# A three-layer graph network on one core: 20 instead of 18 node blocks of layer 1 by count matrices

## The chip, the cores and the metric

The kernel runs on one core of a Trainium2 chip. The metric is the time of one execution on the device, in microseconds (us). A core has five engines with one instruction queue each: PE multiplies matrices, DVE and ACT work on rows of elements, POOL here issues the indirect transfers (gathers), SP and ACT issue the plain ones. An engine carries out its instructions in the order in which they were written and waits for others by semaphores.

## What is computed

Three graph convolutions on 6250 nodes with 256 features and 100,000 edges, sorted by destination, then a residual and a layer norm. With a self loop at each node, `deg` counts the edges that end in a node:

```python
dinv = jnp.where(deg > 0, jax.lax.rsqrt(deg), 0.0)
norm_edge = dinv[src] * dinv[dst]
h = x
for W, b in ((W1, b1), (W2, b2), (W3, b3)):
    # _gcn_layer
    h = h @ W
    msg = h[src] * norm_edge[:, None]
    agg = jax.ops.segment_sum(msg, dst, num_segments=n_nodes)
    h = jax.nn.relu(agg + b)
return _layernorm(x + h)
```

The widths are 256 -> 512 -> 512 -> 256. The kernel sums over the edges first and multiplies by the weights after that, where this is narrower.

## The kernel before, in words

**Blocks and chunks.** The nodes are cut into 50 blocks of `Q` = 125. The edges that end in a block (some 2000) are `KF` = 16 chunks of 128 edges; what goes beyond is gathered once per ten blocks. The sum of a block's incoming rows is made in one of two ways.

*Gathered.* For each chunk, POOL gathers 128 rows of the layer's table from DRAM into a row buffer (L853). PE multiplies them with a 0/1 matrix `shot` of 128 edges by 125 nodes (L879), which DVE makes by comparison, four chunks at a time (L822). For a part of the chunks the row is split into a rounded half (ACT, L894) and the rest (DVE, L897), so that one faster matmul does the work; in layer 1 that is every second chunk. L866 starts a block: it adds the block's own rows (the self loop).

*Dense.* A block's incoming edges are counted in a matrix of 125 destinations by 6250 sources, held as bytes. ACT (in layer 3 at times DVE) converts five 125x125 pieces at a time (L830), and PE multiplies all 50 pieces with the nodes' features, which stay on chip as `parts`, 512 wide (L922). L913 starts such a block.

**Layers.** `layer(i, ...)` writes out one layer, step by step; a step is one chunk of the gathered blocks. Layer 1 (i = 0) gathers blocks `FEW` to 49 and has the first `FEW` = 18 dense. Layer 2 (i = 1) gathers all 50. Layer 3 gathers 22 and has `MANY` = 28 dense. With the gathers per ten blocks, these are 516, 805 and some 354 steps. Each step writes out, in this order: the gather of a chunk, the split of the chunk before it and of one further back, the product of the chunk `lag` = 4 steps back, whatever finishing steps of blocks (`after1` to `after3`) have come due, then the extras (below), then as many dense matmuls as the step's share. In layer 1 the dense share is spread evenly by `spacing` from step 28 to 12 steps before the end: 1.89 matmuls a step.

**Making count matrices.** `counts` makes the matrices from the edges in groups of five destination nodes, 25 groups (`GB`) to a block. For a group, PE multiplies two 0/1 matrices (L727) and ACT copies the product, 125x250, out of PSUM into the byte matrix (L732). The 0/1 matrices come from three comparisons on DVE for five groups together (L705). After the 25th group the matrix is stored to DRAM in `kept` (SP). `fetching_few` fetches it back when two earlier ones are used up, and marks it usable ten steps later. Layer 1 makes the matrices that it uses itself; the other ten (18 to 27) are made in layer 2, a new one every 74 steps. `counts` is a generator; every `yield` ends its share of a step. The argument `rush` is `GB` in layer 1 and 0 in layer 2: in layer 1 the first 25 groups go two to a step, all others, and all in layer 2, one to a step.

**PSUM.** The product of a group goes to one of three places in turn, `mat_places`: two halves of the bank `mat_ps`, and the upper half of the bank `near`. The lower half of that bank is `near_cols`, a table of numbers that DVE reads in all comparisons (L705 and L822).

**Edge windows.** While layer 1 begins, `windows` fetches the edges for the groups, 125 groups at a time, with small operations on DVE, PE, ACT and POOL.

**Row buffers.** In layer 1 there are 25 for the chunks, so POOL can issue that far ahead of their use.

Layer 2 gathers from the table that the finished blocks of layer 1 write, so its first gather waits for the last of them.

Of the kernel before, what the change touches and what calls it, by code (L numbers as in the profile page):

```python
# [37 lines left out]
SPLIT = ((1, 2, 4), (1, 2, 4), (3, 4, 6))  # L38


FEW = 18
MANY = 28
G = 5
GB = Q // G
# [6 lines left out]
def by_rows(queue, tile_rows, dram_rows, store=False):  # L51

    for s in (slice(0, EVEN), slice(EVEN, Q)):
        if store:
            queue.dma_start(out=dram_rows[s], in_=tile_rows[s])
        else:
            queue.dma_start(out=tile_rows[s], in_=dram_rows[s])
# [320 lines left out]
def sorted_path(ctx: ExitStack, tc: tile.TileContext, x, edges, starts, found, wts, biases, room, late, out):  # L378
# [318 lines left out]
    def counts(blocks, places, rush=0):  # L697

        def compared(out, numbers):
            shape = list(out.shape)
            nc.vector.tensor_tensor(out, near_cols[:, :shape[2]].unsqueeze(1).to_broadcast(shape),  # L705
                                    numbers.unsqueeze(2).to_broadcast(shape), op=ALU.is_equal)

        hot = {}
        total = len(blocks) * GB
        for s in range(total + 5):  # L710
            if s < total and s % GB == 0:
                while (blocks[s // GB] + 1) * GB > seen * Q:
                    yield 1
            if s < total and s % WIDE == 0:
                t, w = divmod(blocks[s // GB] * GB + s % GB, Q)
                hot_lo = pairs.tile([P, WIDE, Q], BF16, name="hot_lo")
                hot_key = pairs.tile([P, WIDE, G * NB], BF16, name="hot_key")
                hot[s // WIDE] = hot_lo, hot_key
                compared(hot_lo, slots[:, t, 0, w:w + WIDE])
                compared(hot_key[:, :3], slots[:, t, 1, w:w + 3])  # L720
            if s < total and s % WIDE == 2:
                t, w = divmod(blocks[s // GB] * GB + s % GB + 1, Q)
                compared(hot[s // WIDE][1][:, 3:], slots[:, t, 1, w:w + WIDE - 3])
            m = s - 4
            if 0 <= m < total:
                hot_lo, hot_key = [h[:, m % WIDE] for h in hot[m // WIDE]]
                nc.tensor.matmul(mat_places[m % 3], lhsT=hot_lo, rhs=hot_key, start=True, stop=True)  # L727
            m = s - 5
            if 0 <= m:
                n, u = divmod(m, GB)  # L730
                place = places[n % len(places)]
                nc.scalar.copy(place[:, :, u * G:(u + 1) * G], mat_places[m % 3].rearrange("p (k r) -> p k r", r=G))  # L732
                if u == GB - 1:
                    by_rows(nc.sync, place.rearrange("p k v -> p (k v)"), kept[blocks[n]], store=True)
                    stored.append(blocks[n])
            if s >= rush or s % 2:
                yield 1


# [328 lines left out]
    now = 0  # L1068
    few, many, every = list(range(FEW)), list(range(MANY)), list(range(NB))

    seen = 2

    def steps(b):

        return (NB - b) * KF + NG - b // GRP

    def all_windows():
        nonlocal seen
        for t in range(seen, NW):
            yield from windows(t)  # L1080
            seen += 1

    def fetching_few():

        for m, b in enumerate(few):
            while b not in stored or finished < m - 1:
                yield 1
            fetch(b, now + 10)

    first = 28  # L1090
    spacing = (steps(FEW) - first - 12) / FEW
    layer(0, C, every[FEW:], few, after1, first_rows, first, spacing, [(0, all_windows()), (1, counts(few, (made, also_made), GB)), (1, fetching_few())])

    def last_weights():
        load_w2()
        load_w3()
        yield 1
# [3 lines left out]
    split = two.enter_context(tc.tile_pool(name="swide_split", bufs=4))  # L1101
    gap = (steps(0) - 60) // (MANY - FEW)
    layer(1, HID, every, [], after2, wide_rows,
          extras=[(5, last_weights())] + [(10 + gap * n, counts([b], (made,))) for n, b in enumerate(many[FEW:])])
    there.clear()
    fetch(many[0], 6)
# [189 lines left out]
```

## Time and profile before

| | |
|---|---|
| median of 3 runs | 2350.66 us (2350.42 to 2360.2) |
| the profiled execution | 2345.07 us, span 2343.4 us |
| PE busy (matmul) | 1995.7 us, 85% of the span |
| POOL busy | 1668.6 us, 71% |
| DVE busy | 1540.3 us, 66% |
| ACT busy | 1253.3 us, 53% |
| first gather of layers 1, 2, 3 | 97.58, 796.62, 1873.57 us |
| last gather of layer 1 | 776.13 us |

By stage, busy time of each engine inside a stretch well within layers 1, 2 and 3, from the view of windows:

| stretch, us | PE | DVE | ACT | POOL | DMA share |
|---|---|---|---|---|---|
| 150 to 700 | 484.28 | 378.39 | 347.79 | 402.75 | 0.58 |
| 850 to 1800 | 821.28 | 626.03 | 489.93 | 727.89 | 0.78 |
| 1900 to 2300 | 393.87 | 292.94 | 231.97 | 305.64 | 0.69 |

A line of a group reads: source line, engine, operation, output<-inputs, shape, count, then busy time and mean duration of one in ns, then the engine's idle time ahead of it and what ended that. A line of a timeline reads: start, duration, engine, line, operation, output<-inputs, shape, count, and in brackets the idle time before it and its releaser. A matmul's duration includes its way through the array, so matmuls that follow each other overlap, and the duration of one is more than its price in a row of many. Lines that begin with a time, a duration and an engine with a tile but no operation are from the chain of waits: there the duration is the time that passed on the chain.

### The profile page before, as it was taken

The numbers are of one execution on the slowest core, as the hardware profiler recorded it, in microseconds if no ns is written. First come the engines' busy times: TensorE is split into PE (matmuls) and PEld (weight loads), VectorE is DVE, ScalarE is ACT, GpSimd is POOL, SyncE is SP. The second block draws the span as 40 slices with busy tenths as digits, with TensorE's granted clock in tenths as the row PEclk, the third lists the DMA queues.
The fourth block names the chain that finished last, engine by engine and source line by source line (L and its number), as shares of the span: only waits on it lengthen the run. The fifth ranks groups of instructions, "written<-read, shape, count | busy, mean of one in ns | idle before, by whom it ended". The sixth has DMA issues, their size and how long they took to land.

```text
span 2343.4 us, 29386 instructions
## 1 busy us (share of the span) xinstructions
PE 1995.7 (85%) x7965; PEld 1377.6 (59%) x7965; DVE 1540.3 (66%) x2923; ACT 1253.3 (53%) x2777; POOL 1668.6 (71%) x1716
## 2 busy tenths in 40 slices
PE   3378889889889778988879888898889889999997
PEld 2256656566657335555546555555555667777785
DVE  5677766667664466676666766767665357777776
ACT  1456566666665355555555555545554355555664
POOL 2277677777767577777777777777777377777776
PEclk9989999999999889999999999998999989999998
DMA  8355565566555577777777877777777556676664
GB/s 182 109 152 147 163 192 161 170 181 175 149 165 152 148 228 224 228 235 221 235 226 226 236 221 237 220 228 237 217 232 222 150 154 171 185 184 183 180 181 131
DMA packets 178080, 447.61 MB, mean 191 GB/s; under 512 B 43347, under 2 KB 75429, under 8 KB 177904
## 3 DMA queue, kind: packets, MB, share of 16 engines
q0 software_dynamic: 107456, 326.24, 49.0%
q1 hardware_dynamic: 55328, 107.63, 15.8%
q10 hardware_dynamic: 15120, 11.77, 2.0%
q8 instruction: 64, 1.05, 0.2%
q14 instruction: 112, 0.92, 0.1%
HBM read 391.61 MB, written 53.88 MB: 190 GB/s over the span
## 4 chain that ended last, share of the span: by engine, by line
PE 41%; DMA 25%; DVE 13%; issue 8%; ACT 6%; POOL 4%; ACTq 0%; POOLq 0%; DVEq 0%; SPq 0%
DMA room<-tab,ssrc 16%; PE sacc L879 13%; PE sacc L922 10%; DMA spare<-tab,ssrc 8%; PE smm L969 3%; DVE hot_key L705 3%; DVE halves L897 3%; PE mat_ps L922 3%; PE win_ps L922 3%; ACT halves L894 3%; POOL room L853 3%; PE win_ps L1009 3%; DVE shot L822 2%; PE smm L1026 2%; DVE hot_lo L705 1%
## 5 line engine op out<-in xcount | busy, mean ns | idle before, releaser
L853 POOL DMA_INDIRECT room<-tab,ssrc x1032 | 1016.5, 985 | 317.3 <-issue 138.9
L879 PE MATMUL sacc<-halves,shot 128*125 128x512 f32 x1808 | 734.8, 462 | 82.5 <-DVE halves L897 50.3
L853 POOL DMA_INDIRECT spare<-tab,ssrc x632 | 617.8, 978 | 198.8 <-issue 87.1
L897 DVE TENSOR_TENSOR halves<-room,halves 128x512 fp32r<-128x512 f32 (+1 forms) x746 | 417.4, 565 | 379.9 <-ACT halves L894 368.2
L894 ACT CAST halves<-room 128x512 fp32r<-128x512 f32 (+1 forms) x746 | 381.5, 518 | 341.5 <-DMA room<-tab,ssrc 229.2
L879 PEld LDWEIGHTS sacc<-halves,shot 128*125 128x125 f32 x1808 | 331.5, 192 | 328.1 <-DVE halves L897 110.3
L922 PE MATMUL sacc<-parts,piece 125*125 125x512 f32 x1400 | 476.3, 431 | 10.1 <-ACT piece L830 10.1
L897 DVE TENSOR_TENSOR halves<-spare,halves 128x256 fp32r<-128x256 f32 (+1 forms) x462 | 248.4, 544 | 213.0 <-ACT halves L894 204.6
L879 PE MATMUL sacc<-room,shot 128*125 128x512 f32 (+1 forms) x780 | 332.3, 509 | 11.8 <-DMA room<-tab,ssrc 11.7
L822 DVE TENSOR_TENSOR shot<-near_cols,sdlo 128x500 fp32r<-128x500 f32 x443 | 297.6, 672 | 45.7 <-ACT room L732 23.4
L894 ACT CAST halves<-spare 128x256 fp32r<-128x256 f32 (+1 forms) x462 | 229.2, 503 | 180.5 <-DMA spare<-tab,ssrc 131.2
L922 PEld LDWEIGHTS sacc<-parts,piece 125*125 125x125 f32 x1400 | 236.2, 190 | 92.8 <-issue 30.6
L830 ACT CAST piece<-room 125x625 fp32r<-125x625 uint8 x376 | 268.1, 714 | 41.4 <-DVE piece L830 10.3
L732 ACT CAST room<-mat_ps 125x250 uint8<-125x250 f32 x470 | 197.6, 438 | 167.4 <-PE mat_ps L727 165.7
L705 DVE TENSOR_TENSOR hot_key<-near_cols,slots 128x750 bf16<-128x750 f32 (+1 forms) x280 | 224.2, 801 | 14.7 <-ACT room L732 8.5
L1009 PE MATMUL win_ps<-room,w_sb 128*128 128x250 f32 x800 | 212.2, 390 | 1.6 <-ACT room L1017 0.9
L727 PEld LDWEIGHTS <-hot_lo 128*125 128x125 bf16 x700 | 98.9, 142 | 172.8 <-DVE hot_key L705 102.8
L1009 PEld LDWEIGHTS win_ps<-room,w_sb 128*128 128x128 f32 x800 | 160.4, 201 | 49.6 <-issue 23.7
L732 ACT CAST room<-near_cols 125x250 uint8<-125x250 f32 x230 | 100.7, 438 | 146.3 <-DVE hot_key L705 86.5
L879 PEld LDWEIGHTS sacc<-room,shot 128*125 128x125 f32 x780 | 144.4, 195 | 46.8 <-DMA room<-tab,ssrc 14.1
L727 PE MATMUL near_cols<-hot_key,hot_lo 128*125 128x250 bf16 x230 | 67.8, 295 | 115.0 <-DVE hot_key L705 87.7
L727 PE MATMUL mat_ps<-hot_key,hot_lo 128*125 128x250 bf16 x470 | 131.0, 281 | 11.5 <-ACT room L732 11.3
(181 smaller groups left out, 1985.7 us busy)
## 6 DMA issues: line engine op xcount, KB each, us to landing
room<-kept SPq DMA_DIRECT2D x46, 683.6 KB
kept<-room SPq DMA_DIRECT2D x28, 683.6 KB
tab<-st SPq DMA_DIRECT2D x75, 224.0 KB
room<-tab,ssrc POOLq DMA_INDIRECT x1032
spare<-tab,ssrc POOLq DMA_INDIRECT x632
spare<-tab SPq DMA_DIRECT2D x43, 224.0 KB
out<-st ACTq DMA_DIRECT2D x50, 112.0 KB
room<-in_x ACTq DMA_DIRECT2D x4, 1120.0 KB
```

The costliest lines, as they stand in the source:

```text
L705: nc.vector.tensor_tensor(out, near_cols[:, :shape[2]].unsqueeze(1).to_broadcast(shape), numbers.unsqueeze(2).to_broadcast(shape), op=ALU. ...
L727: nc.tensor.matmul(mat_places[m % 3], lhsT=hot_lo, rhs=hot_key, start=True, stop=True)
L732: nc.scalar.copy(place[:, :, u * G:(u + 1) * G], mat_places[m % 3].rearrange("p (k r) -> p k r", r=G))
L822: nc.vector.tensor_tensor(hot[:, :n], near_cols[:, :Q].unsqueeze(1).to_broadcast([P, n, Q]), dlo.rearrange("p b j -> p (b j)")[:, at:at + ...
L830: convert(piece, used[m % 2][:, c * PIECE:(c + 1) * PIECE, :])
L853: nc.gpsimd.indirect_dma_start(out=row, out_offset=None, in_=tables[i], in_offset=bass.IndirectOffsetOnAxis(ap=at, axis=0))
L879: nc.tensor.matmul(acc[:Q, :size], lhsT=hot, rhs=row[:, c0:c0 + size], start=(i == 1 and k == c0 == 0), stop=(k == KF and c0 + size == row ...
L894: nc.scalar.copy(halves[:, :width], landed[chunk - hi_lag])
L897: nc.vector.tensor_sub(halves[:, width:], landed.pop(chunk - lo_lag), halves[:, :width].bitcast(F32))
L922: nc.tensor.matmul(acc_d[:Q], lhsT=got[done // PIECE][:, k % PIECE, :], rhs=parts[:, k], start=False, stop=(k == NB - 1))
L969: nc.tensor.matmul(y_ps, lhsT=zt[:, k, :], rhs=w1_sb[:, k, :], start=(k == 0), stop=(k == KC - 1))
L1009: nc.tensor.matmul(h_ps[:, f, :], lhsT=w2_sb[:, k, (f2 + f) * P:(f2 + f + 1) * P], rhs=zt2[:, k, :], start=(k == 0), stop=(k == KH - 1))
```

## The change

Two blocks of layer 1 move from the gathered to the dense way (`FEW`), and with them the making of their two count matrices moves from layer 2 to layer 1. In layer 1, from the 26th group on, a step carries a second group whenever the group's number is a multiple of eight, so that eight groups go in seven steps. Layer 1 has 483 steps and 20 dense blocks, 2.26 dense matmuls a step; layer 2 makes eight matrices, one every 93 steps. Layer 3 is as before.

```diff
-FEW = 18
+FEW = 20
 MANY = 28
...
     def counts(blocks, places, rush=0):
...
                 if u == GB - 1:
                     by_rows(nc.sync, place.rearrange("p k v -> p (k v)"), kept[blocks[n]], store=True)
                     stored.append(blocks[n])
-            if s >= rush or s % 2:
+            if s % 2 if s < rush else s % 8 or not rush:
                 yield 1
```

The places where `FEW` counts, unchanged:

```python
first = 28
spacing = (steps(FEW) - first - 12) / FEW
layer(0, C, every[FEW:], few, after1, first_rows, first, spacing, [(0, all_windows()), (1, counts(few, (made, also_made), GB)), (1, fetching_few())])
...
gap = (steps(0) - 60) // (MANY - FEW)
layer(1, HID, every, [], after2, wide_rows,
      extras=[(5, last_weights())] + [(10 + gap * n, counts([b], (made,))) for n, b in enumerate(many[FEW:])])
```

## The prediction

> **What bounds the kernel now.** I read the chain and the groups of the page first, and they name the gathers: POOL's indirect DMAs are the costliest group, and gathered rows head the chain of waits. So I took the time per stage, in the timeline of POOL.
>
> ```profile
> L853 POOL DMA_INDIRECT room<-tab,ssrc x1032 | 1016.5, 985 | 317.3 <-issue 138.9
> ...
> 415.43 0.95 POOL L853 DMA_INDIRECT room<-tab,ssrc  x1 [0.30 <-PE mat_ps L727]
> 416.68 0.94 POOL L853 DMA_INDIRECT room<-tab,ssrc  x1 [0.30 <-DVE hot_key L705]
> ...
> 641.70 0.94 POOL L853 DMA_INDIRECT room<-tab,ssrc  x1 [1.48 <-PE mat_ps L727]
> ```
>
> A gather is issued every 1.25 us and each carries 0.30 us of fixed gap, whatever releaser is named. In layers 2 and 3 no gather waits longer than that 0.31 us (the first ones apart), so POOL sets their pace. In layer 1 some do wait, for PE, between 618 and 710 us. POOL runs up to 25 row buffers ahead there; a wait means that the buffers are used up and PE is the slower one. PE's own pace is read from its timeline at L866, the first matmul of each gathered block:
>
> ```profile
> 134.54 0.77 PE L866 MATMUL sacc<-parts,ident_r 125*125 125x512 f32 x1
> 157.67 0.40 PE L866 MATMUL sacc<-parts,ident_r 125*125 125x512 f32 x1
> ...
> 706.52 0.39 PE L866 MATMUL sacc<-parts,ident_r 125*125 125x512 f32 x1
> 723.22 0.39 PE L866 MATMUL sacc<-parts,ident_r 125*125 125x512 f32 x1
> ...
> 774.64 0.40 PE L866 MATMUL sacc<-parts,ident_r 125*125 125x512 f32 x1
> ```
>
> The first and the third line are 26 blocks apart: 572.0 / 26 = 22.0 us a block, while POOL needs 16.1 x 1.25 = 20.1 us. From 706.52 to 774.64 it is 4 blocks in 68.1, 17.0 us each. What ends at 708 us is the making of count matrices (L727's last matmul there). So while counts are made, the layer goes at PE's pace, and the counts cost 5.0 us per block of 16.1 groups: 0.31 us a group. Bare, a count matmul takes 0.11 to 0.24 us on PE (chain of waits, 178.60 and 179.83 us). The rest is waiting, and the groups by form from 150 to 700 us say where:
>
> ```profile
> L727 PE MATMUL mat_ps<-hot_key,hot_lo 128*125 128x250 bf16 x270 | 73.5, 272 | 1.7 <-ACT room L732 1.5
> L727 PE MATMUL near_cols<-hot_key,hot_lo 128*125 128x250 bf16 x135 | 38.9, 288 | 41.2 <-DVE hot_key L705 35.6 <-DVE shot L822 4.0 <-ACT room L732 0.8
> ```
>
> Two of the three places of a count product lie in mat_ps and wait for nothing; the third shares a bank with near_cols, which DVE reads in every comparison, and there PE loses 41.2 of the roughly 66 us that it idles in these 550. That bank ties PE, DVE and ACT together once every three groups.
>
> The Trainium skill says of this (PSUM — Partial Sum Buffer, "PSUM bank collisions raise a hardware error") that the scheduler adds a dependency between any two instructions on different engines that touch one bank and quadrant, reads against reads too, even at different columns. The trace agrees as far as it goes, with 41.2 us of waiting at that place against 1.7 at the two others. By that rule the wait belongs to the group, not to the block, and the sum is the first of the two below (+27); without it the second (+18) would be as good.
>
> **The change, part by part.** Times are of the profiled execution (span 2343.4, 2345.07 us in all), which is 5.6 us under the median of the runs shown, 2350.66.
>
> *Removed from layer 1:* two gathered blocks, 33 gathers (483 steps instead of 516). At POOL's 1.25 that is 41 us of issuing, but POOL is not the bound while counts are made, so what counts is PE's share. *Added:* 2 dense blocks of 50 matmuls, 50 count groups, one group more per seven steps. In the order of the built program a gathered block then carries 18.4 count groups and 36.2 dense matmuls instead of 16.1 and 30.4, and the counts end 25.6 blocks after the block that starts at 134.54, with 2.4 left, instead of 26 and 4.
>
> Prices on PE, from the chain where nothing holds it:
>
> ```profile
> 180.31 1.72 PE smm L969 x4
> 182.03 0.23 PE sacc L913
> 182.26 0.24 PE sacc L922
> ```
>
> A dense matmul 0.235, times 5.8 = 1.36 us a block. Its bounds are 0 (it fills a wait) and the 0.44 of its mean duration in this stage; I take the bare one, since PE issues it back to back. The finishing of dense blocks: 0.72 instead of 0.61 per gathered block, each 4 x 0.43 + 2 x 0.19 + 0.23 = 2.3 us, so +0.25. A count group 0.31, with 0.11 (bare) below and 0.84 above (before any dense block runs, the block from 109.29 to 134.54 takes 25.2 us for 30 groups, two per step; there DVE is the limit). I take 0.31, as the rows of this very stage give it.
>
> A block with counts after: 17.0 + 1.36 + 0.25 + 18.4 x 0.31 = 24.3 us; without: 18.6. From 134.54 to the start of the last block: 25.6 x 24.3 + 2.4 x 18.6 = 667 us, against 640 now: +27. The 22 us from there to the first gather of layer 2 (774.64 to 796.62) stay. If the waits stay as they are per block and only the bare 0.11 to 0.24 of each further group is added, a block takes 22.0 + 1.61 + 2.3 x 0.15 = 23.96 and it is +18. I take the middle, **+22 us**.
>
> *Moved out of layer 2:* 50 groups, some 7 us of count matmuls on PE and 50 casts on ACT. Costed at nothing, since gathers pace that layer; in the windows the first and the third stretch have 20 count matmuls each, the others none:
>
> ```profile
> 1005.00:1035.00 30.00, 22.99 (x24) 0.94 0.73 207
> 1050.00:1080.00 30.00, 22.70 (x25) 0.94 0.78 234
> 1105.00:1135.00 30.00, 23.28 (x23) 1.00 0.75 217
> 1150.00:1180.00 30.00, 22.99 (x24) 0.94 0.78 229
> ```
>
> POOL issues 24, 25, 23 and 24 gathers in 30 us (columns: busy, count, PE clock, DMA share, GB/s). Were the difference of one gather real, 10 stretches of some 35 us would hide about 14 us, and two fewer are worth 3. The spread also comes from where the window cuts; I keep 0 to -3.
>
> *Queues:* SP gets two stores and two fetches of matrices more in layer 1 and two stores fewer in layer 2, 0.75 us of issuing each. Behind them in order stand the stores of finished rows, which layer 2 alone reads. What can hurt is lateness: a matrix must be stored, fetched and landed before ACT converts its first piece, and ACT, then PE, would stand still for it. Now this slack grows from 10 steps for the first matrix to over 30; after, it stays at 10 to 17 (a matrix is made in 21.9 steps and used in 22.15). In the timeline of SP a store at 164.99 is followed by its fetch at 169.43, and the first piece is converted at 177.87: at most 13 us, under 10 steps x 1.4. Cover is thin, price 0; a fetch that is held up behind other stores (306.99 to 315.68) would miss by about 4 us, and some eight matrices have no more slack: up to +30.
>
> Layer 3 and the start are not touched. Sum: 2345 + 22 = 2367 on the profiled execution, 2373 on the median; I write 2371.
>
> **The rivals.**
> 1. *Gathers pace layer 1 after all* (or a block with counts still takes 22.0 us): 33 x 1.25 = 41 us less, or 25.6 x 22.0 + 2.4 x 17.0 = 604 instead of 640, 36 less: about 2311. It decides once a block with counts takes less than 20.1 us on PE. For it: the page's chain and POOL's group. Against: PE lags POOL by all buffers from 618 us on, and blocks take 17.0 us as soon as counts stop.
> 2. *The added work fills PE's waits.* PE idles 66 of 550 us, 2.6 us a block; if the added 2.0 us go half into it, a block takes 23.0 and the sum is 25.6 x 23.0 + 2.4 x 18.6 = 633, 7 less: about 2341. For it: DVE is late at the shared bank, and gets more time per step. Against: DVE also gets 14% more comparisons per step, and work per three groups hardly changes on any engine (three groups then span 2.62 steps instead of 3).
> 3. *The doubled step hurts*, or the fetches come late: in every eighth group two products follow each other with only one cast between them, two of the three places being one bank. At 0.84 us for such a group instead of 0.31, 60 of them add 32 us: 2403. For it: the block at 109.29. Against: there DVE also makes windows.
> 4. *No change of the work*: excluded, the built program has 33 gathers fewer, 500 count matmuls in layer 1 and 200 in layer 2.
>
> **How the numbers follow.** Forecast 0.59, rival 1 0.13, rival 2 0.17, rival 3 0.11. A change under 0.5% (12 us) is not told from none here: within that lie rival 2 and a little of the forecast's lower edge, 0.19; faster is rival 1 and a rest, 0.14; slower 0.67. The range holds the forecast with both prices of a group, rival 2 with a larger share filled (another 5 us), and rival 3: 2338 to 2402. Rival 1 is left out. The likeliest alone: 2360 to 2388.
>
> **What would show it.** L866 in PE's timeline about 24 us apart until some 750 us and 18 to 19 after; the first gather of layer 2 near 818 instead of 796.62; waits of POOL for PE from early in layer 1, near 60 us in all (33 x 1.25 + 22); idle time of near_cols L727 up by a tenth. Layers 2 and 3 as long as now: 1076.9 us from first gather to first gather, and 469.8 from 1873.57 to the end. Wrong if blocks stay at 22 us (rival 1), if near_cols idles less while blocks take 23 (rival 2), if waits appear on mat_ps or before L830 (rival 3), or if layer 2 changes its length by more than 5 us.

## The result and the profile after

The changed kernel takes 2373.19 us (median of 8 runs, 2363.61 to 2381.18) against 2353.41 us of the kernel before (8 runs beside it, 2350.42 to 2360.2): a ratio of 1.0082 with a 95% interval of 1.0059 to 1.0105, or +19.8 us. The profiled execution took 2374.55 us. The page of the kernel after gives its span and the busy time, share and instructions of each engine:

```profile
span 2372.9 us, 29390 instructions
PE 2018.6 (85%) x8013; PEld 1384.6 (58%) x8013; DVE 1532.3 (65%) x2899; ACT 1262.1 (53%) x2781; POOL 1645.3 (69%) x1683
```

PE's share is 85%, as before, so this part of the page tells nothing. The stages do. From the timeline of POOL in the kernel after, the first gather that waited for PE, the last gather of layer 1, and the first of layers 2 and 3:

```profile
416.80 1.00 POOL L853 DMA_INDIRECT room<-tab,ssrc  x1 [1.14 <-PE mat_ps L727]
...
789.77 1.11 POOL L853 DMA_INDIRECT room<-tab,ssrc  x1 [0.31 <-issue]
818.63 0.95 POOL L853 DMA_INDIRECT room<-tab,rest  x1 [27.75 <-issue]
...
1899.33 0.95 POOL L853 DMA_INDIRECT room<-tab,rest  x1 [30.55 <-DMA tab<-st]
```

With the first gather of all at 97.40, the stages of the two profiled executions are:

| us | before | after | difference |
|---|---|---|---|
| first gather of layer 1 to that of layer 2 | 699.0 | 721.2 | +22.2 |
| layer 2 to layer 3 | 1076.9 | 1080.7 | +3.8 |
| layer 3 to the end | 469.8 | 473.5 | +3.7 |

The change does nothing in layer 3, so I take the 3.7 us there for what such a stage varies by from one execution to the next, and layer 2's 3.8 can't be told from it. The spans of these two executions differ by 29.5 us and the medians by 19.8, so I take layer 1's 22.2 as known to some 4 us, not to tenths. The loss is in layer 1. PE's timeline at L866, the first matmul of each gathered block, after:

```profile
134.94 0.48 PE L866 MATMUL sacc<-parts,ident_r 125*125 125x512 f32 x1
...
739.74 0.40 PE L866 MATMUL sacc<-parts,ident_r 125*125 125x512 f32 x1
758.19 0.40 PE L866 MATMUL sacc<-parts,ident_r 125*125 125x512 f32 x1
776.41 0.40 PE L866 MATMUL sacc<-parts,ident_r 125*125 125x512 f32 x1
796.94 0.39 PE L866 MATMUL sacc<-parts,ident_r 125*125 125x512 f32 x1
```

The first two lines are 25 blocks apart: 604.8 / 25 = 24.19 us a block with counts, where it was 22.0. The three blocks behind take 18.45, 18.2 and 20.5 us, 19.1 on average, where it was 17.0.

POOL's side of the same layer is a ledger, from the start times of its gathers: their number less one times the median distance, the waiting beyond that, and the time from the last gather to the first of layer 2.

| us | issuing | waiting | last gather to layer 2 | sum |
|---|---|---|---|---|
| before | 515 x 1.251 = 644.3 | 34.3 | 20.5 | 699.0 |
| after | 482 x 1.254 = 604.4 | 87.9 | 28.9 | 721.2 |

Two blocks less to gather took 40 us of issuing away; 54 us of waiting came in, and 8 at the end. The waits view of POOL from 100 to 800 us names for whom it waited, after (total, times, longest in us; 0.3 of each is the fixed gap of a gather):

```profile
POOL w_sb L464 <- DVE w_sb L461: 22.5, 4, 10.2
POOL spare L853 <- PE sacc L879: 16.5, 19, 2.5
...
POOL room L853 <- PE sacc L879: 15.1, 18, 2.5
POOL room L853 <- PE mat_ps L727: 12.7, 15, 2.7
POOL spare L853 <- PE near_cols L727: 11.7, 13, 2.1
```

All lines of this view that name PE sum to 87.1 us over 119 waits; without the gap, 51 us. In the kernel before it is 49.1 over 131, so 10 us. The row buffers are used up from 417 us on instead of 618: PE lags from there. The first line is a wait of the edge windows' fetches, which stand in POOL's queue between the gathers; it was 11.7 us.

### The profile page after: what moved, and what is told of

Read it like the earlier page. It is cut to its first block, busy times and chain, and to the rows that moved or that the text cites. A ratio compares the mean times of both kernels' runs of the same rounds, so it can differ in the third digit from the quotient of the medians.

```text
span 2372.9 us, 29390 instructions
## 1 busy us (share of the span) xinstructions
PE 2018.6 (85%) x8013; PEld 1384.6 (58%) x8013; DVE 1532.3 (65%) x2899; ACT 1262.1 (53%) x2781; POOL 1645.3 (69%) x1683
## 4 chain that ended last, share of the span: by engine, by line
DMA 26%; PE 25%; DVE 7%; issue 6%; ACT 5%; POOL 3%; ACTq 0%; SPq 0%; POOLq 0%; DVEq 0%
DMA room<-tab,ssrc 17%; PE sacc L879 8%; DMA spare<-tab,ssrc 8%; PE sacc L922 5%; PE mat_ps L922 3%; ACT halves L894 3%; DVE halves L897 3%; PE win_ps L922 2%; PE win_ps L1009 2%; POOL room L853 2%; PE smm L1026 1%; DVE shot L822 1%; DVE hot_key L705 1%; PE smm L969 1%; POOL spare L853 1%
## 5 line engine op out<-in xcount | busy, mean ns | idle before, releaser
L853 POOL DMA_INDIRECT room<-tab,ssrc x1016 | 1008.8, 993 | 336.4 <-issue 142.1
L853 POOL DMA_INDIRECT spare<-tab,ssrc x616 | 603.0, 979 | 213.2 <-issue 76.8
L897 DVE TENSOR_TENSOR halves<-room,halves 128x512 fp32r<-128x512 f32 (+1 forms) x790 | 449.5, 574 | 389.1 <-ACT halves L894 383.2
L894 ACT CAST halves<-room 128x512 fp32r<-128x512 f32 (+1 forms) x790 | 410.3, 526 | 413.3 <-DMA room<-tab,ssrc 288.0
L897 DVE TENSOR_TENSOR halves<-spare,halves 128x256 fp32r<-128x256 f32 (+1 forms) x402 | 208.6, 524 | 224.7 <-ACT halves L894 213.0
L822 DVE TENSOR_TENSOR shot<-near_cols,sdlo 128x500 fp32r<-128x500 f32 (+1 forms) x435 | 291.6, 670 | 41.6 <-ACT room L732 26.4
L922 PEld LDWEIGHTS sacc<-parts,piece 125*125 125x125 f32 x1500 | 252.4, 190 | 98.0 <-issue 36.2
L830 ACT CAST piece<-room 125x625 fp32r<-125x625 uint8 x396 | 282.1, 714 | 40.7 <-DVE halves L897 9.4
L879 PE MATMUL sacc<-room,shot 128*125 128x256 f32 (+1 forms) x656 | 269.7, 494 | 11.1 <-DMA room<-tab,ssrc 11.1
L894 ACT CAST halves<-spare 128x256 fp32r<-128x256 f32 (+1 forms) x402 | 193.0, 488 | 141.2 <-DMA spare<-tab,ssrc 99.3
L705 DVE TENSOR_TENSOR hot_key<-near_cols,slots 128x750 bf16<-128x750 f32 (+1 forms) x280 | 224.1, 801 | 20.9 <-ACT room L732 13.0
L727 PEld LDWEIGHTS <-hot_lo 128*125 128x125 bf16 x700 | 96.7, 140 | 157.9 <-DVE hot_key L705 91.2
L879 PE MATMUL sacc<-spare,shot 128*125 128x256 f32 (+1 forms) x428 | 180.9, 505 | 2.5 <-DMA spare<-tab,ssrc 2.4
L727 PE MATMUL near_cols<-hot_key,hot_lo 128*125 128x250 bf16 x230 | 67.2, 292 | 101.2 <-DVE hot_key L705 75.6
L879 PEld LDWEIGHTS sacc<-room,shot 128*125 128x125 f32 x656 | 122.0, 195 | 39.7 <-DMA room<-tab,ssrc 12.0
```

Source lines behind the costliest of these rows:

```text
L822: nc.vector.tensor_tensor(hot[:, :n], near_cols[:, :Q].unsqueeze(1).to_broadcast([P, n, Q]), dlo.rearrange("p b j -> p (b j)")[:, at:at + ...
L830: convert(piece, used[m % 2][:, c * PIECE:(c + 1) * PIECE, :])
L853: nc.gpsimd.indirect_dma_start(out=row, out_offset=None, in_=tables[i], in_offset=bass.IndirectOffsetOnAxis(ap=at, axis=0))
L879: nc.tensor.matmul(acc[:Q, :size], lhsT=hot, rhs=row[:, c0:c0 + size], start=(i == 1 and k == c0 == 0), stop=(k == KF and c0 + size == row ...
L894: nc.scalar.copy(halves[:, :width], landed[chunk - hi_lag])
L897: nc.vector.tensor_sub(halves[:, width:], landed.pop(chunk - lo_lag), halves[:, :width].bitcast(F32))
```

## The experiments

The expectations name their theories by letters and say what each holds and what it gives.

### First set: the parts of the change, and the shared bank taken away

Four kernels on one chip, on which the kernel before takes 2348.23 us (7 runs, 2347.57 to 2352.33), four timed runs each. Layer lengths are read from first gather to first gather, as above.

**few18_double**: only the faster pace of the groups; 18 blocks as before. The work is that of the kernel before.

```diff
-            if s >= rush or s % 2:
+            if s % 2 if s < rush else s % 8 or not rush:
```

> FEW = 18 as before, only the yield of the change (eight groups in seven steps). Theory W (layer 1 goes by the work written for PE and DVE, 0.31 us per count group, whatever step it stands in): the same 450 groups, 900 dense matmuls and 516 gathers, so layer 1 keeps its length, 699 us from its first gather to layer 2's first, within 5; blocks with counts take 22.7 us instead of 22.0 and counts end some 50 steps earlier; total within 6 us of before. Rival D (a doubled step costs by itself, 0.84 instead of 0.31 us for the second group): 53 doubled steps add 28 us, layer 1 near 727.

Measured: 2372.1 us, a ratio of 1.0095 (1.0078 to 1.0112); layer 1 took 726.7 us, layer 2 1078.4, layer 3 470.2. The faster pace alone, with no block moved, costs as much as the whole change, or a little more. Theory D had 727 us for layer 1, theory W 699. PE's timeline and that of POOL in few18_double:

```profile
134.75 0.47 PE L866 MATMUL sacc<-parts,ident_r 125*125 125x512 f32 x1
...
676.63 0.39 PE L866 MATMUL sacc<-parts,ident_r 125*125 125x512 f32 x1
...
794.19 0.40 PE L866 MATMUL sacc<-parts,ident_r 125*125 125x512 f32 x1
...
806.89 0.95 POOL L853 DMA_INDIRECT room<-tab,ssrc  x1 [0.30 <-issue]
823.94 0.94 POOL L853 DMA_INDIRECT room<-tab,rest  x1 [16.10 <-issue]
```

The counts end at 672 us instead of 709. Until then there are 23 blocks of 541.9 / 23 = 23.56 us, then 7 of 16.8. Against the kernel before: 23 x (23.56 - 22.0) = +36 while counts are made; three blocks that no longer carry counts, and the four that never did, 7 x 16.8 - 3 x 22.0 - 4 x 17.0 = -16; and the end is 7.7 us longer (29.7 instead of 22.0 from the last block's start). That sums to 27.7, the measured difference. The end shows why being done with the counts early brought so little back: the last block starts at 794.19, but its last gather only at 806.89, while in the kernel before the last gather (776.13) is issued 1.5 us after the last block's start. POOL had stood 65.4 us in all (34.3 before), and issues back to back from there; PE, at 16.8 us a block, caught up with it and then had to wait for the last rows. What POOL loses early it can't make up.

At the shared bank, groups by form from 150 to 650 us in few18_double, and below it the same of the kernel before:

```profile
L727 PE MATMUL mat_ps<-hot_key,hot_lo 128*125 128x250 bf16 x261 | 68.1, 271 | 4.7 <-ACT room L732 4.5
L727 PE MATMUL near_cols<-hot_key,hot_lo 128*125 128x250 bf16 x131 | 38.2, 292 | 52.3 <-DVE hot_key L705 44.8 <-DVE shot L822 5.1 <-ACT halves L894 1.5
```

```profile
L727 PE MATMUL mat_ps<-hot_key,hot_lo 128*125 128x250 bf16 x246 | 66.9, 272 | 0.5 <-ACT room L732 0.4
L727 PE MATMUL near_cols<-hot_key,hot_lo 128*125 128x250 bf16 x124 | 35.9, 289 | 37.2 <-DVE hot_key L705 31.6 <-DVE shot L822 4.0 <-ACT room L732 0.8
```

A product in the shared bank waits 52.3 / 131 = 0.40 us instead of 37.2 / 124 = 0.30. Eight groups now share seven steps, and the comparisons on DVE come due sooner, but PE gets the product not much sooner: from one product in this bank to the next, PE takes on average 3.82 us instead of 4.06, 6% less for 14% more groups per step.

**few19_single**: one block more is dense, at the old pace.

```diff
-FEW = 18
+FEW = 19
```

> FEW = 19 with the old yield, one group a step: half of the moved blocks and no doubled step. W: 25 groups and 50 dense matmuls more, 16 gathers fewer: half of the change's 22 us, layer 1 near 710 us, total some 11 us over before. D: the loss of the change comes from the doubled steps; without them the fewer gathers show, layer 1 at 699 or below. Gathers set the pace: 16 x 1.25 = 20 us less, 679.

Measured: 2383.66 us, 1.0148 (1.0117 to 1.018), layer 1 742.9 us. The theories had 710, 699 and 679, so none had this, and it doesn't tell them apart: at one group a step a matrix is ready every 25 steps, while 19 dense blocks use one every 24.2. In PE's timeline the dense matmuls come evenly until some 548 us, 30 to 37 in each gathered block, and then in bursts, from 15 to 51, with several blocks of 26 to 29 us. So more than 18 dense blocks need a faster pace, and the two parts of the change can't be taken apart on this side; 20 blocks at the old pace need 488 steps for their 500 groups (the first 25 go in 13), and there are 483.

**few18_sbuf** and **few20_sbuf**: the table `near_cols` lies in SBUF, and the third place of a product no longer shares a bank with anything that DVE reads; the first with the rest as before, the second with the whole change.

```diff
+    near_cols = const.tile([P, G * NB], F32, name="near_sb")
...
-    near_cols = near[:, :G * NB]
```

> Before, but the table near_cols that DVE compares with lies in SBUF, so DVE no longer reads the PSUM bank in which every third group's product is made. W with the tie at that bank: the 41 us that near_cols L727 idles between 150 and 700 us fall under 10, a block with counts takes 20.1 to 20.6 us (POOL's pace or just over) instead of 22.0, layer 1 is 30 to 40 us shorter, about 663. Rival L (DVE is late by its load, the bank is only where it shows): the idle time moves to the other L727 and to LDWEIGHTS, a block stays at 21.5 to 22.5. If comparisons take longer from SBUF, DVE's rows show it and the gain shrinks by that much; layers 2 and 3 stay within 5 us in either case.

> After, with near_cols in SBUF in the same way. W with the tie: a block with counts takes some 22.5 us instead of 24.2, layer 1 is 40 us shorter than after's 721, about 680, and still longer than few18_sbuf's, since PE has 23 us of bare work more in it. L: a block stays near 24. Rival F (work fills waits once the tie is gone): both SBUF kernels run at POOL's pace and this one, with 33 gathers fewer, is the shorter by up to 41 us.

Measured: few18_sbuf 2434.41 us, 1.0364 (1.0347 to 1.0381), layer 1 739.8, layer 2 1117.0; few20_sbuf 2394.96 us, 1.0186 (1.0166 to 1.0206), layer 1 706.7, layer 2 1117.8. No forecast of these lengths held: layer 1 was to be near 663 and near 680, and layer 2 within 5 us of before. The groups by form from 150 to 650 us, few18_sbuf and then few20_sbuf:

```profile
L727 PE MATMUL mat_ps<-hot_key,hot_lo 128*125 128x250 bf16 x235 | 65.5, 279 | 22.9 <-ACT room L732 22.6
L727 PE MATMUL near_cols<-hot_key,hot_lo 128*125 128x250 bf16 x118 | 32.6, 277 | 4.3 <-ACT room L732 4.2
```

```profile
L727 PE MATMUL mat_ps<-hot_key,hot_lo 128*125 128x250 bf16 x266 | 69.9, 273 | 17.5 <-ACT room L732 17.1
L727 PE MATMUL near_cols<-hot_key,hot_lo 128*125 128x250 bf16 x133 | 36.5, 274 | 0.7 <-ACT room L732 0.7
```

The wait for DVE is gone, so it was the bank and not DVE being late by its load: few20_sbuf makes a product at the third place every 3.76 us, more often than any kernel with the shared bank, and still waits only 0.7 us there. Part of the wait comes back at the two other places, where PE now waits for ACT's casts. The gain doesn't show, because something else became slower; the groups of POOL in the same stretch, few18_sbuf and then the kernel before:

```profile
L853 POOL DMA_INDIRECT room<-tab,ssrc x185 | 201.9, 1091 | 56.4 <-issue 23.5 <-DMA room<-tab,ssrc 8.5 <-PE sacc L922 4.6
```

```profile
L853 POOL DMA_INDIRECT room<-tab,ssrc x198 | 189.1, 955 | 61.5 <-issue 31.4 <-PE sacc L879 5.8 <-PE mat_ps L727 4.2
```

A gather takes 1.09 us on POOL instead of 0.96, and in both kernels no gather of rows (L853) in layer 1 but the first waits over 0.4 us: gathers pace this layer 1, and layer 2 too, which is 40 us longer. In that regime moving two blocks pays: few20_sbuf's layer 1 is 33.1 us shorter than few18_sbuf's, 1.0 us for each of the 33 gathers that it doesn't make. It is also 14.5 us shorter than that of the changed kernel, though every gather costs more. F, that the added work fits in once the tie is gone, holds here. The prediction's first rival is right for these two kernels; whether for want of the tie or because each gather takes longer, they don't separate.

### Second set: another way out of the bank, on other chips

Here the kernel before takes 2794.07 us (24 runs, 2780.31 to 2809.01) in one series and 2801.59 (25 runs, 2784.44 to 2813.52) in the other: the first set ran on chip 0 and these series on chips 2 and 4, which are 19% slower with the same kernel. There is no profile of the kernel before or after from them. So only kernels within this set are compared, by their ratios to the kernel before and by the length of layer 1. Why these chips are slower isn't known. PE's granted clock is 0.87 to 0.90 on average in their eight profiles and 0.92 to 0.96 in the other six; DVE's instructions last as long as on the first chip (the 750-wide comparison 928 ns in few17, 929 in the kernel before). In few17's layer 1 PE waits 64 us ahead of L727 without anything named that it waited for; the profile of the kernel before has no such wait. The longest stretch in which all five engines stand is under 5 us in all eight traces, not 20 as one expectation below has it; single engines do wait some 20 (ACT 20.3 in few17).

**few18_win**, **few18_double_win**, **few20_win**: once the edge windows are fetched (at 415 to 431 us in these traces, in the tenth gathered block), the third product goes to the bank `win_ps`, which the windows used until then, and the table stays where it is; with the kernel before, with the faster pace alone, and with the whole change.

```diff
+        at = {}
...
-                nc.tensor.matmul(mat_places[m % 3], lhsT=hot_lo, rhs=hot_key, start=True, stop=True)
+                if m % 3 == 2 and rush and seen == NW:
+                    at[m] = ps_mat.tile([P, 512], F32, name="win_ps")[:Q, :G * NB]
+                else:
+                    at[m] = mat_places[m % 3]
+                nc.tensor.matmul(at[m], lhsT=hot_lo, rhs=hot_key, start=True, stop=True)
...
-                nc.scalar.copy(place[:, :, u * G:(u + 1) * G], mat_places[m % 3].rearrange("p (k r) -> p k r", r=G))
+                nc.scalar.copy(place[:, :, u * G:(u + 1) * G], at.pop(m).rearrange("p (k r) -> p k r", r=G))
```

**few17**: one dense block less than before (`FEW = 17`), else as before.

> FEW = 17 with the old yield, no doubled step: the move of blocks alone, turned round by one. Theory W (the added work sets the price, some 11 us a block moved): 11 us less than before, layer 1 near 688 us from first gather to first gather. Theory D (the doubled steps set the price, the move itself costs about nothing, as FEW = 18 with the doubled steps was already 22 us over before and after is the same): layer 1 within 5 us of before's 699, or up to 6 longer where the 17 more gathers begin to bind.

> Before, but once the edge windows are fetched (some 150 steps in) the third place of a count product is the bank of win_ps, which is idle by then, instead of the bank that DVE compares from; nothing else moves. Theory B (the tie of PE, DVE and ACT at that bank makes the waits): L727 at the third place idles less than 0.05 us each instead of 0.30, blocks from the ninth on fall from 22.0 to POOL's 20.1 or little over, layer 1 is 12 to 25 us shorter, 674 to 687. Rival L (DVE is late by its load): the idle time moves to the other places, blocks stay at 21.5 to 22.5, layer 1 within 5 us of 699.

> The doubled steps with FEW = 18 and the third place in the bank of win_ps. B: the doubled step costs because it meets that bank more tightly, so most of its price goes: within 8 us of few18_win, layer 1 under 695. Rival A (a doubled step costs since two casts of ACT and two products follow each other in the halves of mat_ps): some 15 to 20 us stay over few18_win, and mat_ps L727 idles more.

> After, with the third place in the bank of win_ps. B: blocks from the ninth on fall from 24.2 to 22.5 or less, layer 1 is 25 to 35 us shorter than after's 721, 686 to 696, the total some 2345, under before. L: blocks stay at 24, total 2370. If the added work is free once the tie is gone, it is also shorter than few18_win, since it has 33 gathers fewer.

All four were run a second time, in the other series:

> As few17. W: layer 1 near 688 us, 11 less than before. D: 699 within 5, or up to 6 longer where more gathers bind.

> The same kernel as few18_win, since the chip of that run was 440 us slower with every kernel, before too, with stalls of 20 us at which all engines stand. B: layer 1 at 674 to 687 us instead of before's 699, blocks from the ninth on 20.1 to 20.7; L: within 5 us of 699.

> As few18_double_win. B: within 8 us of few18_win_b, layer 1 under 695 instead of few18_double's 727. A: 15 to 20 us over few18_win_b.

> As few20_win. B: layer 1 at 686 to 696 us instead of after's 721, total some 2345, under before's and 25 to 30 under after's; still shorter if the added work is free without the tie, as on the slower chip, where it was 46 us under before and few18_win 9 under. L: total 2370.

| | ratio to before, first series | second series | layer 1, us |
|---|---|---|---|
| few17 | 1.0066 (1.004 to 1.0091) | 1.0034 (1.0009 to 1.006) | 885.1, 888.0 |
| few18_win | 0.9979 (0.9956 to 1.0003) | 0.9955 (0.9926 to 0.9983) | 864.5, 866.7 |
| few18_double_win | 1.0009 (0.9981 to 1.0037) | 0.9992 (0.9963 to 1.0021) | 881.1, 879.7 |
| few20_win | 0.9831 (0.9786 to 0.9877) | 0.9825 (0.9775 to 0.9874) | 837.2, 835.2 |

The faster pace alone still costs: few18_double_win's layer 1 is 13 to 17 us longer than few18_win's, near the 15 to 20 us that theory A gave. But the place is not A's. The starts of the tenth and the last gathered block (L871 is L866 here) in few18_win, and below it in few18_double_win:

```profile
414.48 0.39 PE L871 MATMUL sacc<-parts,ident_r 125*125 125x512 f32 x1
...
939.97 0.40 PE L871 MATMUL sacc<-parts,ident_r 125*125 125x512 f32 x1
```

```profile
432.00 0.40 PE L871 MATMUL sacc<-parts,ident_r 125*125 125x512 f32 x1
...
955.23 0.40 PE L871 MATMUL sacc<-parts,ident_r 125*125 125x512 f32 x1
```

The faster pace is 17.5 us behind at the tenth block, while the third product still goes to the shared bank, and no more from there on: 523.2 us to the last block against 525.5 (in the other series 14 us behind, then 525.6 against 527.2). So here the pace costs nothing that can be seen once the third product has its own bank. That need not hold on the first chip: behind the counts a block still takes 22 to 23 us in these two kernels, where it was 17.0, so on these chips something other than PE's work sets the pace. B's forecast of the blocks failed as well: from the tenth on they take 24.2 us in few18_win, not 20.1 to 20.7, and 24.5 to 24.8 in few20_win, not 22.5. The groups by form of few20_win from 500 to 780 us show where PE waits now:

```profile
L732 PE MATMUL mat_ps<-hot_key,hot_lo 128*125 128x250 bf16 x140 | 37.1, 274 | 16.3 <-ACT room L737 10.6 <-issue 3.3 <-ACT halves L899 1.7
L732 PE MATMUL win_ps<-hot_key,hot_lo 128*125 128x250 bf16 x70 | 19.7, 282 | 2.7 <-ACT room L737 1.5 <-issue 1.2
```

In its own bank the third product waits 2.7 us for 70, and the two in `mat_ps` 16.3 for 140, for ACT above all. On top of this pace two more dense blocks bring 44 us, and few20_win is 1.7% faster than the kernel before on these chips. It was not run on the first chip, nor the changed kernel on these, so whether few20_win beats the kernel before where the prediction was made stays open. A block less by counts makes few17, which keeps the shared bank, 0.3 to 0.7% slower than before, 11 to 16 us: theory W, which had it 11 us shorter, fails here. By an estimate from that price two blocks more bring 22 to 32 of the 46 to 53 us by which few20_win is under the kernel before, so much of its gain on these chips may have nothing to do with the bank.

## Why the prediction was right, and which of its steps were not

*Direction, place and size.* Right: +22 us were forecast in layer 1 and +22.2 came; 2373 on the median was the sum, 2371 was written, and it is 2373.19. That it agrees to a fraction of a us is luck: the medians differ by 19.8 us, and the runs after span 17.6. The kernel's layer 1 goes at PE's pace, and taking 33 gathers from POOL gave nothing. The first rival would have shown blocks of 22 us; they took 24.19, with 24.3 forecast, and 19.1 with 18.6 forecast behind the counts.

*POOL's waits* for PE are 51 us, near 60 forecast. *Layers 2 and 3* are within 4 us, with layer 3 untouched; 50 groups fewer in layer 2 bring nothing that can be seen, as forecast. The windows of the kernel after in layers 1 and 2 (busy time and count of PE, PEld, DVE, ACT, POOL, then clock, DMA share and GB/s):

```profile
150.00:700.00 550.00, 483.22 (x2137) 338.66 (x2136) 368.87 (x664) 352.37 (x882) 367.92 (x383) 0.99 0.55 158
850.00:1800.00 950.00, 823.02 (x2952) 518.14 (x2953) 609.34 (x936) 479.25 (x934) 728.05 (x729) 0.96 0.77 226
```

POOL's 728 us of 950 in layer 2 are those of before (727.89): its gathers pace that layer with or without the groups. In layer 1 PE is as busy as before (484.28), and POOL 35 us less. The *price 0 for late matrices* held: dense matmuls waited 0.5 us in all for L830 from 150 to 650 us.

*The step that failed is the split of the sum.* The prediction priced 2.3 further groups per block at 0.31 us each (+0.71) and the further dense work at its bare price (1.36 + 0.25 = +1.61). few18_double has the first without the second: +1.56 per block, or 0.68 us for a further group. That is near the 0.84 of the third rival, but not by its mechanism: its sign, waits at mat_ps, came to 4.7 us (0.5 before), and the wait that grew most is the one at the shared bank, 52.3 us instead of 37.2. (Its total, 2403, also lies 1 us outside the range that was said to hold it.) From few18_double to the changed kernel the dense work then adds 24.19 - 23.56 = 0.63 us per block, so that 1.0 of its 1.61 us filled waits, as the second rival said of half of it. Two terms were off by 0.85 and 0.98 us in opposite directions, and that the sum, 2.19 against 2.32, came out right is luck. The terms are taken in this order because the other, dense work at the old pace, can't be run. The groups by form of the kernel after, 150 to 700 us, show where most of the dense work went:

```profile
L727 PE MATMUL mat_ps<-hot_key,hot_lo 128*125 128x250 bf16 x280 | 73.6, 273 | 3.6 <-ACT room L732 3.4
L727 PE MATMUL near_cols<-hot_key,hot_lo 128*125 128x250 bf16 x139 | 39.9, 287 | 40.1 <-DVE hot_key L705 30.2 <-DVE shot L822 3.8 <-ACT halves L894 1.6
```

40.1 / 139 = 0.29 us of waiting per product in the shared bank, where few18_double has 0.40. At 6.1 such products per block, that is 0.7 us of the 1.0 filled. The forecast sign "near_cols idles a tenth more" failed for the same reason: 40.1 us against 41.2. The rule of the Trainium skill that the prediction draws on (PSUM — Partial Sum Buffer, "PSUM bank collisions raise a hardware error") stands as far as the wait goes: with the table out of the bank it fell from 37.2 to 4.3 us. But the wait did not stay with the group at a fixed price: it is 0.30 us a product before, 0.40 with the pace alone and 0.29 after. I read it as what is left over between DVE's pace and PE's other work; no run shows that by itself.

So the loss comes from the pace that 20 dense blocks force on the counts, and on top of it the two moved blocks cost nothing more: layer 1 takes 721.2 us with both and 726.7 with the pace alone. That the tie at the shared bank makes the pace dear on the first chip is shown in part: its waits grew there, and without it (few20_sbuf) the layer is shorter in spite of slower gathers. On the slower chips the pace cost 14 to 17 us up to the tenth block, with the tie, and nothing behind it, without. How much of the 27.7 us of few18_double is the tie, and how much ACT's casts, isn't settled: no run on the first chip takes the tie away and leaves the gathers as they are.

## What to carry to other kernels

When a change needs one engine's work to come at a faster pace, price the pace by itself, with a kernel that has it and nothing else: here it was the whole loss, though its work was the same. Read a stage's pace from the starts of its blocks, and then make the ledger of the engine that seems to be the bound (issuing, waiting, end); what it gets back on the one line it may lose on the next. A sum that comes out right doesn't show that its terms are, and two errors of the same size stood in this one.

## What was not expected of the hardware

With `near_cols` in SBUF, DVE's comparisons took as long as before (the 750-wide one 935 ns instead of 929), but 85 of 356 gathers from 150 to 650 us took over 1.2 us on POOL, against 1 of 382 in the kernel before; the median stayed at 0.95. The Trainium skill (SBUF — State Buffer, "SBUF: two separate sides") says that a DVE operation with two inputs in SBUF and a GpSimd operation that reads SBUF hold a pair of ports exclusively, so that the later one waits. The trace agrees: the table was the one input outside SBUF, and 72 of the 85 slow gathers start while one of the comparisons (L705, L822) runs, against 59 of the 271 others. Moving the table cost 40 us in layer 2, where gathers set the pace. Slow gathers were there already in the kernel before: of 65 between 850 and 1800 us, 60 start while L897 runs, whose two inputs lie in SBUF, against 241 of the 664 others.

The same kernel takes 2348 us on one chip and 2794 and 2802 us on two others. Whether the change would rank the same there wasn't tried.
